# Moving three pieces at the two ends of layer 1: transposes of the second batch, the last norms and the range check

## The chip, the cores and the metric

The kernel runs on one core of a Trainium2 chip. The metric is the device time of one execution in microseconds. Engines are TensorE (PE; its weight loads PEld), VectorE (DVE), ScalarE (ACT), GpSimd (POOL) and SyncE (SP), which issues the DMAs here. Each engine works through its own queue in order and waits on semaphores that other engines raise.

## The reference

Two layers over x of shape (16, 1024, 256), all in float32. Layer 0 aggregates with a normalized adjacency matrix, applies two linear maps with batch norms, adds x and layer-normalizes. Layer 1, in which the change lies, is this, per batch, and a residual and a layer norm behind it:

```python
    def _L1_gnn_ref(x, para, adj, kv_w):
        B, N, C = x.shape
        ...
        c_adj = jnp.mean(fea, axis=1)
        diff = c_adj[:, None, :] - c_adj[:, :, None]
        A = jnp.abs(jnp.abs(jax.nn.sigmoid(diff) - 0.5) - 0.5) * 2.0
        A_s = (A + jnp.transpose(A, (0, 2, 1))) * 0.5
        Wg = adj[None, :, :] * A_s
        g = jnp.einsum('bcn,bnm->bcm', fea, Wg)
        g = jax.nn.relu(g * para.reshape(1, C, N))
        ...
        attn = jax.nn.softmax(jnp.einsum('bhnd,bhmd->bhnm', q, k) * scale, axis=-1)
        out = jnp.einsum('bhnm,bhmd->bhnd', attn, v)
    ...
    x = _layernorm(x + _L1_gnn_ref(x, L1_gnn_para, adj, L1_gnn_kv_w), axis=-1)
```

With q from the graph product g, k and v from x @ kv_w, and 4 heads of 64.

## The kernel before

Layer 0 ends at about 820 us; the rest is `fast()`, layer 1. Its order is written out in program order by a small planner, and each engine's queue follows that order.

**Steps and slots.** Attention of one batch is 16 steps: 2 halves of the queries (`hf`, 512 each), 2 pairs of heads, 4 groups of 256 keys. A step is `scores` (L783, TensorE), `exps` (L795, ScalarE), `sums` (L801, L804, VectorE, the softmax denominators' accumulator) and `attend` (L819, TensorE). With B = 16 that is steps 0 to 255. Two steps make a slot, so a batch has NC = 8 slots. `put(w, t, f, ...)` hangs a piece of side work on slot 8w + t, and the loop at the end (L1123) takes two slots at a time: first all pieces of both, in the order that `arrange` gives them, then four steps, with the scores and exponentials one step ahead. Pieces for batch b + 1 or b + 2 (norms, keys, values, graph product) hang on the slots of batch b. Slots -8 to -1 come before the first attention step; there `opening` also emits `gate0` and `graph0`, the gates and the graph product of batch 0, whose last call emits the four `queries`, which read the graph product from the two PSUM buffers of `ps_s`.

**First end (batch 1 in slots -8 to -1).** For each of four row blocks j: `load` (SP), `bn2_q` (POOL), `rows` and `ln1_a` (VectorE, then POOL), `ln1_b` (ScalarE, L642). `x1_t(1, j)` then transposes the block by four TensorE transposes (L671, tile `px`) and copies it on VectorE (L672, into `x1T`) for the keys and values of batch 1. `means` (L675, L677) and `crow` follow: `crow` transposes the row means (L692, tile `pc`), copies them (L694), and sends them through DRAM (L695, L696) to come back as a row on all partitions; the gates of batch 1 (`wg_a`, L706) read that row. `px`, `pc`, keys, values and the attention outputs share the four buffers of the pool `ps_t`.

**Last end (batch 15).** When a half is done, `dens` (L846, L848) and `recips` (L857, L859) make the reciprocals. `finish_a(15, j)` (L888 to L901) brings block j back to rows, scales it, adds the residual and takes norm statistics on VectorE and POOL; `finish_b(15, j)` (L909, L912) applies the norm on ScalarE and stores. For the second half (`by_pe`) the transposition back is four TensorE transposes per block (L885, tile `pf`), inside `finish_a`. `range_all` (L928 to L939) checks the range of the denominators: VectorE, a tiny matmul L935, VectorE; a rare general path follows it if the check fails. In the planner these lines set the places:

```python
                    if b == B - 1:
                        t_a, t_b = (t + 2 + k, t + 3 + k) if hf == 0 else (t + 1 + k, t + 2 + k)
```

where t is 4 for the first half and 8 for the second, k is 0 or 1. So before, `finish_b(15, 0)` is in slot 7 of batch 15 (127 over all), ahead of the last group of four steps, and `finish_b(15, 1)` in slot 128, behind them.

Of the kernel before, what the change touches and what calls it, by code (L numbers as in the profile page):

```python
# [9 lines left out]
F32 = mybir.dt.float32  # L10
# [6 lines left out]
P = 128  # L17
# [5 lines left out]
def gnn_norm_attention_kernel(  # L23
# [16 lines left out]
    nc = tc.nc  # L40
    B, N, C = x.shape
# [13 lines left out]
    ident = const.tile([P, P], F32, name="ident")  # L55
# [69 lines left out]
    with ExitStack() as l0:  # L125
# [32 lines left out]
        with ExitStack() as ph1:  # L158
# [9 lines left out]
            for i in range(0, NT, 2):  # L168
                t = hp.tile([P, 2, N], F32, tag="h", name=f"A{i}")
# [22 lines left out]
            KB = FB // P  # L192
# [6 lines left out]
            for h in range(NH):  # L199
# [11 lines left out]
                for j in range(NT):  # L211
                    p = ps.tile([P, FB], F32, tag="ah"[j % 2], name="pat")
# [25 lines left out]
            for c in range(HT):  # L238
                p = ps.tile([P, FB], F32, tag="a", name="pw1")
# [3 lines left out]
            for c in range(CT):  # L243
                p = ps.tile([P, FB], F32, tag="a", name="pw2")
# [142 lines left out]
            for f in range(HT):  # L387
                for h in range(NH):
# [3 lines left out]
                    p = hidden(B - 1, h, f)  # L392
# [57 lines left out]
        with ExitStack() as ph2:  # L450
# [74 lines left out]
            for k, pair in enumerate(pairs):  # L525
# [4 lines left out]
                if not ahead:  # L530
                    for j in range(LDP):
                        load(0, j)
                    for j in range(LDP, NT // 2):
                        t = accp.tile([P, 2, FB], F32, tag="acc", name=f"first{j}")
# [14 lines left out]
    NP = HEADS // 2  # L549
# [17 lines left out]
    def fast():  # L567
      with ExitStack() as fx:
# [13 lines left out]
        ps_t = pool("ps_t", 4, space=PSUM)  # L582

        x1s, x1Ts, css, crows, mvs, wgs = {}, {}, {}, {}, {}, {}
        kTs, qTs, vs, S, E, ACC, O, OT, DT = {}, {}, {}, {}, {}, {}, {}, {}, {}
# [222 lines left out]
        def by_pe(b, hf):  # L808
            return b == B - 1 and hf == NH - 1
# [42 lines left out]
        KB = FB // P  # L852
# [9 lines left out]

        OB = {}

        def fetch_o(b, j):
            hf, k = divmod(2 * j, KB)
            if by_pe(b, hf):
                return
            t = OB[b, j] = otp.tile([P, 2, C], F32, tag="ob", bufs=2, name=f"ob{b}_{j}")
            blk = o_dram[b, hf].rearrange("i (d e) (q n) -> q e (i d) n", e=Q, q=NQ)  # L870
            for q in range(NQ):
                nc.sync.dma_start(
                    t[q * Q : (q + 1) * Q].rearrange("p a (d n) -> p (a d) n", n=Q),
                    blk[q][:, ts(k // 2, 2 * C // Q), :],
                )

        def finish_a(b, j):
            hf, k = divmod(2 * j, KB)
            pool_r = (rp, "r") if b < B - 1 else (x1p, "x1")
            r = pool_r[0].tile([P, 2, C], F32, tag=pool_r[1], name=f"r_{b}_{j}")  # L880
            if by_pe(b, hf):
                p = ps_t.tile([P, 2, C], F32, tag="t", name="pf")
                for a in range(2):
                    for pair in range(NP):
                        nc.tensor.transpose(p[:, a, ts(pair, P)], OT[b, hf, pair][:, ts(k + a, P)], ident)  # L885
            else:
                p = r
                nc.vector.transpose(  # L888
                    r.rearrange("p a c -> p (a c)"), OB.pop((b, j)).rearrange("p a c -> p (a c)")
                )  # L890
            rd = RD[:, b * NT + 2 * j : b * NT + 2 * j + 2, :].rearrange("p a h -> p (a h)")
            nc.vector.tensor_mul(
                r.rearrange("p a (h d) -> p (a h) d", h=HEADS),
                p.rearrange("p a (h d) -> p (a h) d", h=HEADS),
                rd.unsqueeze(2).to_broadcast([P, 2 * HEADS, HD]),
            )
            nc.vector.tensor_add(r, r, x1s.pop((b, j)))
            mv, rs = ln_stats(sm, r, f"z{b}_{j}")
            nm = sm.tile([P, 2], F32, tag="nm", name=f"nm_{b}_{j}")
            for a in range(2):  # L900
                nc.gpsimd.tensor_scalar(  # L901
                    nm[:, a : a + 1], mv[:, a, 0:1], rs[:, a : a + 1], -1.0, op0=OP.mult, op1=OP.mult
                )
            R[b, j] = (r, rs, nm)
# [39 lines left out]
        NC = NS // 2  # L944
        at = {}

        def put(w, t, f, *a):
            at.setdefault(w * NC + t, []).append((f, a))
# [4 lines left out]
        for b in range(B):  # L953

            for hf in range(NH):
                t = (hf + 1) * (NC // NH)
                put(b, t, dens, b, hf)
                put(b, t, recips, b, hf)
                for k in range(KB // 2):
                    j = hf * (KB // 2) + k  # L960

                    t_a, t_b = (t + 2 + k, t + 6 + k) if hf == 0 else (t + 4 + k, t + 6 + k)
                    if b == B - 1:
                        t_a, t_b = (t + 2 + k, t + 3 + k) if hf == 0 else (t + 1 + k, t + 2 + k)
                    put(b, t + 1, fetch_o, b, j)
                    put(b, t_a, finish_a, b, j)
                    put(b, t_b, finish_b, b, j)
            if b == 0:
                continue

            put(b - 2, 2, begin, b)
            for j in range(NT // 2):
                put(b - 2, j, load, b, j)
                put(b - 2, j + 1, bn2_q, b, j)
                put(b - 2, j + 2, rows, b, j)
                put(b - 2, j + 2, ln1_a, b, j)
                put(b - 2, j + 3, ln1_b, b, j)
                if b == 1:
                    put(b - 2, j + 4, x1_t, b, j)
                    continue  # L980
                put(b - 2, j + 3, put_x1, b, j)
                put(b - 2, 5 + j // 2 * 2, get_x1, b, j)
                put(b - 2, min(6 + j, NC), x1_v, b, j)
            put(b - 2, NC - 2, means, b)
            put(b - 2, NC - 1, crow, b)

            i = 0
            for t, n in enumerate(WG):
                for i in range(i, i + n):
                    put(b - 1, t, gate, b, i)  # L990
                i += 1
            kv = [(keys, (b, c, h)) for h in range(NH) for c in range(CT)]
            kv += [(values, (b, j)) for j in range(0, NT, 2)]
            for t, n in enumerate(KV):
                for _ in range(n):
                    f, a = kv.pop(0)
                    put(b - 1, t, f, *a)
            m = 0
            for t, n in enumerate(QG):
                for m in range(m, m + n):  # L1000
                    put(b - 1, NC - len(QG) + t, graph, b, m)
                m += 1
        put(B - 1, 4, range_so_far)
        put(B - 1, NC + 1, range_all)

        nsteps = B * NS


        order = (dens, recips, x1_t, finish_a, fetch_o, finish_b, x1_v, rows, ln1_a, ln1_b, put_x1, get_x1, means, load, crow)
        rank = {f: k for k, f in enumerate(order)}  # L1010
        short = (dens, recips, x1_t)

        def is_short(fa):
            f, a = fa
            return f in short or f is finish_a and by_pe(a[0], 2 * a[1] // KB)

        long = (keys, values, graph)

# [9 lines left out]
        def arrange(pieces):  # L1028
            first = []
            gates = [fa for fa in pieces if fa[0] is gate]  # L1030
            many = [fa for fa in pieces if fa[0] in long]
            first += [fa for fa in pieces if fa[0] is bn2_q]
            alone = [fa for fa in pieces if fa[0] in (dens, recips, crow)]
            few = [fa for fa in pieces if fa not in first + gates + many + alone]
            few.sort(key=lambda fa: rank.get(fa[0], len(rank)))
            few_pe = [fa for fa in few if is_short(fa)]
            order = spread(many, few_pe) if len(many) < len(few_pe) else spread(few_pe, many)
            if few_pe and many and order[0][0] in long:
                order.remove(few_pe[0])
                order.insert(0, few_pe[0])  # L1040

            for fa in few:
                if not is_short(fa):
                    at_ = 0
                    for k, o in enumerate(order):
                        if o[0] in rank and rank[o[0]] <= rank.get(fa[0], len(rank)):
                            at_ = k + 1
                    order.insert(at_, fa)
            if any(fa[0] is graph for fa in many):
                order = gates + order  # L1050
            else:
                order = spread(order, gates)


            for f, k in ((dens, 1), (recips, 2)):
                k = ([n for n, fa in enumerate(order) if fa[0] in long] + [len(order)] * 3)[k]
                order[k:k] = [fa for fa in alone if fa[0] is f]
            return first + order + [fa for fa in alone if fa[0] is crow]


# [62 lines left out]
        for t in range(min(at) // 2, max(max(at) // 2, nsteps // NK - 1) + 1):  # L1123
# [3 lines left out]
            for k in range(len(now) + 1):  # L1127
                if k == behind and 0 <= g < nsteps:
                    sums(g)
                if k < len(now):  # L1130
                    f, a = now[k]
# [15 lines left out]
        )  # L1147

    flag = fast()


# [155 lines left out]
```

## Time and profile before

| | us |
|---|---|
| median of 3 runs | 2494.07 (2491.98 to 2497.5) |
| the profiled execution | 2492.39 |
| its span, first to last instruction | 2490.6 |
| PE busy | 2427.3 (97%) |
| DVE busy | 1798.8 (72%) |
| ACT busy | 1096.0 (44%) |
| POOL busy | 761.9 (31%) |
| mean granted TensorE clock | 0.993 of full |

The profile is of one execution. Times in the views are microseconds from the start of the span; L12 is line 12 of the kernel. A timeline line gives the start, the duration, engine, line, operation, tiles and shapes, the count of instructions merged into it, and in brackets how long the engine had been idle before it and what ended that. A view by windows gives, for each stretch, the busy time of each engine and the granted clock. A float32 matmul is recorded as two.

### The profile page before, as it was taken

The page shows a single profiled execution, that of the slowest core. Times are in us where ns is not written, and L with a number is a line of the kernel's source. Part 1 is how long each engine was busy: PE and PEld are TensorE (multiplying, and loading weights), DVE is VectorE, ACT ScalarE, POOL GpSimd, SP SyncE. Part 2 cuts the span into 40 slices and gives each one's busy share as a digit, 9 for nine tenths or more (in the row PEclk, how much of TensorE's full clock was granted, in tenths as well). Part 3 has the DMA queues.
Part 4 walks back from the last instruction along what each step waited for, and adds up shares of the span by engine and source line. Part 5 has one row for each costly group of instructions (what it writes and reads, how often), then busy time and mean ns, then how long its engine had stood idle before and what let it go on. Part 6 is the DMA issues. An engine that isn't in the chain of part 4 may idle for free. (4 is left out here: it accounts for less than half of the span.)

```text
span 2490.6 us, 33864 instructions
## 1 busy us (share of the span) xinstructions
PE 2427.3 (97%) x12341; PEld 1019.2 (41%) x12341; DVE 1798.8 (72%) x2552; ACT 1096.0 (44%) x1549; POOL 761.9 (31%) x826
## 2 busy tenths in 40 slices
PE   8999999999999799999999999999999999999996
PEld 4444444443444443443434434344344343443432
DVE  5545555555777577888788888888888878887666
ACT  2000000003543455564655656656556465564554
POOL 2222222221656232313223133232341432313002
PEclk9999999999999899999999999999999999999998
DMA  3122222222686443544554535445354455453211
GB/s 135 68 85 102 87 82 85 101 74 78 244 281 226 119 119 82 134 119 111 140 111 110 142 85 146 113 119 145 88 136 111 113 138 111 114 143 87 72 40 40
DMA packets 563118, 288.66 MB, mean 116 GB/s; under 512 B 390664, under 2 KB 535680, under 8 KB 555776
## 3 DMA queue, kind: packets, MB, share of 16 engines
q1 hardware_dynamic: 562944, 286.43, 41.6%
q8 instruction: 99, 1.62, 0.3%
q14 instruction: 75, 0.61, 0.1%
HBM read 192.43 MB, written 93.91 MB: 115 GB/s over the span
## 5 line engine op out<-in xcount | busy, mean ns | idle before, releaser
L795 ACT ACTIVATE e<-s 128x1024 f32<-128x1024 f32 x512 | 496.3, 1021 | 338.9 <-PE s L783 286.9
L804 DVE TENSOR_TENSOR acc<-acc,e 128x1024 f32<-128x1024 f32 x384 | 510.7, 1330 | 119.9 <-ACT e L795 93.3
L783 PE MATMUL s<-qT,kT 64*64 64x512 f32 x4096 | 492.3, 595 | 12.0 <-ACT e L795 8.7
L819 PE MATMUL o<-e,v 64*64 64x512 f32 x4096 | 485.3, 589 | 0.0
L757 PE MATMUL pg<-wg,x 128*128 128x512 f32 x960 | 428.9, 597 | 0.0
L610 POOL TENSOR_TENSOR yt<-yt,stq 128x512 f32<-128x512 f32 x120 | 179.4, 1495 | 430.3 <-DMA yt<-yT 390.3
L819 PEld LDWEIGHTS o<-e,v 64*64 64x64 f32 x4096 | 156.6, 133 | 283.5 <-issue 274.9
L783 PEld LDWEIGHTS s<-qT,kT 64*64 64x64 f32 x4096 | 147.3, 133 | 305.8 <-issue 261.3
L757 PEld LDWEIGHTS pg<-wg,x 128*128 128x128 f32 x960 | 177.5, 190 | 231.4 <-issue 227.5
L103 ACT COPY u<-pa 128x512 f32<-128x512 f32 x15 | 8.8, 586 | 475.3 <-PE pa L308 475.3
L716 DVE SCALAR_TENSOR_TENSOR wg<-wg,adj 128x1024 f32<-128x1024 f32 x128 | 162.9, 1302 | 4.0 <-ACT wg L709 1.2
L66 POOL TENSOR_SCALAR rs_z<-mv_z 128x2 f32<-128x2 f32 x64 | 16.9, 265 | 482.7 <-DVE mv_z L559 401.6
L308 PE MATMUL pa<-AhT,x 128*128 128x512 f32 x360 | 161.8, 592 | 0.0
L642 ACT ACTIVATE x<-x,nm_a,rs_a 128x256 f32<-128x256 f32 x128 | 75.8, 594 | 177.9 <-POOL nm_a L632 177.5
L831 DVE TENSOR_TENSOR ot<-o,ot 128x512 f32<-128x512 f32 x64 | 44.3, 692 | 149.8 <-ACT ot L830 149.8
L732 PE MATMUL pk<-x1T,kvw 128*128 128x512 f32 x256 | 122.2, 612 | 1.3 <-DVE x1T L672 1.3
L743 PE MATMUL pv<-kvw,x1T 128*128 128x256 f32 x512 | 117.1, 382 | 0.0
L66 POOL TENSOR_SCALAR rs_a<-mv_a 128x2 f32<-128x2 f32 x64 | 38.8, 606 | 252.9 <-DVE mv_a L559 233.5
L339 PE MATMUL ph<-agg,SW 128*128 128x512 f32 x240 | 112.8, 592 | 0.0
L743 PEld LDWEIGHTS pv<-kvw,x1T 128*128 128x128 f32 x512 | 96.0, 190 | 31.5 <-issue 16.5
L308 PE MATMUL pa<-T,sx 128*128 128x512 f32 x240 | 107.9, 592 | 0.0
L308 PEld LDWEIGHTS pa<-AhT,x 128*128 128x128 f32 x360 | 68.4, 190 | 86.1 <-issue 86.1
(192 smaller groups left out, 3155.1 us busy)
## 6 DMA issues: line engine op xcount, KB each, us to landing
adj<-in_adj_dram SPq DMA_DIRECT2D x128, 512.0 KB, 4.4
h<-hT SPq DMA_DIRECT2D x28, 1024.0 KB, 4.4
hL<-h SPq DMA_DIRECT2D x28, 1024.0 KB, 9.7
x<-in_x_dram SPq DMA_DIRECT2D x16, 1024.0 KB, 7.2
yT<-y SPq DMA_DIRECT2D x64, 256.0 KB, 2.5
out_dram<-r SPq DMA_DIRECT2D x64, 256.0 KB, 2.3
xr<-in_x_dram SPq DMA_DIRECT2D x62, 256.0 KB, 3.6
o<-ot SPq DMA_DIRECT2D x62, 256.0 KB, 2.3
```

Source lines behind the costliest of these rows:

```text
L308: nc.tensor.matmul(p, xs[n][:, k, :], bs[n][:, k, :], start=(k == 0), stop=(k == KN - 1))
L339: nc.tensor.matmul(p, ws[n][:, ts(f, P)], bs[n], start=True, stop=True)
L610: nc.gpsimd.tensor_tensor(y, y, sc, op)
L642: nc.scalar.activation(r, r, AF.Identity, bias=nm[:, a : a + 1], scale=rs[:, a : a + 1], accum_out=css[b][:, i : i + 1])
L716: nc.vector.scalar_tensor_tensor(t, t, 1.0, adjs[b * NT + i], op0=OP.add, op1=OP.mult)
L732: nc.tensor.matmul(p, kvw[:, k, ts(c, P)], x1Ts[b][:, k, ts(h, FB)], start=(k == 0), stop=(k == CT - 1))
L743: nc.tensor.matmul(p[:, ts(a, C)], x1Ts[b][:, k, ts(j + a, P)], kvw[:, k, C:], start=(k == 0), stop=(k == CT - 1),)
L757: nc.tensor.matmul(pg[b], x1s[b, k // 2][:, k % 2, ts(c, P)], wgs[b, k][:, ts(h, FB)], start=(k == 0), stop=(k == NT - 1))
L783: nc.tensor.matmul(t[r * HD : (r + 1) * HD, h, :], kTs[b, pair][h * HD : (h + 1) * HD, ts(2 * cb + r, HD)], qTs[b, pair, hf][h * HD : (h + ...
L795: nc.scalar.activation(E[g, a], S.pop((g, a)), AF.Exp)
L804: nc.vector.tensor_add(ACC[b, hf, pair], ACC[b, hf, pair], E[g, a])
L819: nc.tensor.matmul(O[b, hf, pair][r][h * HD : (h + 1) * HD, :], vs[b][r * HD : (r + 1) * HD, cb, pair * P + h * HD : pair * P + (h + 1) * HD],
```

## The change

Four things move, and nothing is added to or taken from the computation. `x1_t(1, j)` for all four blocks moves to slot -1, behind the last graph matmuls and the queries of batch 0. The transposes of `finish_a` for the last half become a piece of their own, `back`, which stands directly behind `dens` and ahead of `recips`. `finish_b(15, 0)` and `finish_b(15, 1)` move to slot 9 of batch 15 (129), behind all attention. `range_all` moves from slot 9 to slot 10, behind the last `finish_a`. Lines of the kernel after L870 are two to five higher in the changed one.

```diff
+        def back(b, j):
+            hf, k = divmod(2 * j, KB)
+            p = OB[b, j] = ps_t.tile([P, 2, C], F32, tag="t", name="pf")
+            for a in range(2):
+                for pair in range(NP):
+                    nc.tensor.transpose(p[:, a, ts(pair, P)], OT[b, hf, pair][:, ts(k + a, P)], ident)
+
         def fetch_o(b, j):
             hf, k = divmod(2 * j, KB)
-            if by_pe(b, hf):
-                return
...
             if by_pe(b, hf):
-                p = ps_t.tile([P, 2, C], F32, tag="t", name="pf")
-                for a in range(2):
-                    for pair in range(NP):
-                        nc.tensor.transpose(p[:, a, ts(pair, P)], OT[b, hf, pair][:, ts(k + a, P)], ident)
+                p = OB.pop((b, j))
...
                     if b == B - 1:
-                        t_a, t_b = (t + 2 + k, t + 3 + k) if hf == 0 else (t + 1 + k, t + 2 + k)
-                    put(b, t + 1, fetch_o, b, j)
+                        t_a, t_b = (t + 2 + k, NC + 1) if hf == 0 else (t + 1 + k, t + 2 + k)
+                    put(b, t if by_pe(b, hf) else t + 1, back if by_pe(b, hf) else fetch_o, b, j)
...
                 if b == 1:
-                    put(b - 2, j + 4, x1_t, b, j)
+                    put(b - 2, NC - 1, x1_t, b, j)
...
-        put(B - 1, NC + 1, range_all)
+        put(B - 1, NC + 2, range_all)
...
-        short = (dens, recips, x1_t)
+        short = (dens, recips, x1_t, back)
...
-            return f in short or f is finish_a and by_pe(a[0], 2 * a[1] // KB)
+            return f in short
...
-            alone = [fa for fa in pieces if fa[0] in (dens, recips, crow)]
+            alone = [fa for fa in pieces if fa[0] in (dens, back, recips, crow)]
...
-            for f, k in ((dens, 1), (recips, 2)):
+            for fs, k in (((dens, back), 1), ((recips,), 2)):
                 k = ([n for n, fa in enumerate(order) if fa[0] in long] + [len(order)] * 3)[k]
-                order[k:k] = [fa for fa in alone if fa[0] is f]
+                order[k:k] = [fa for fa in alone if fa[0] in fs]
```

In the built program this gives, at the first end, on TensorE: all 64 records of the graph, four times four transposes L671, L692, scores of step 0; on VectorE: `means`, the eight query instructions, four L672. At the last end, on TensorE: L846, eight transposes, L857; on VectorE: the reciprocal, two `finish_a`, the range check; on ScalarE: L848, then eight L909. The orders of POOL and SP are the same as before.

## The prediction

> **What bounds the kernel now.** I read the page first, then layer 1 by long windows, then the timeline at its two ends. The page and the windows say where time can be won at all:
>
> ```profile
> PE 2427.3 (97%) x12341; PEld 1019.2 (41%) x12341; DVE 1798.8 (72%) x2552; ACT 1096.0 (44%) x1549; POOL 761.9 (31%) x826
> ...
> 900.00:1300.00 400.00, 399.61 (x2556) 162.14 (x2548) 321.47 (x435) 227.50 (x315) 118.89 (x151) 1.00 0.47 115
> ...
> 2100.00:2454.00 354.00, 352.08 (x2390) 139.41 (x2386) 269.69 (x355) 202.84 (x268) 77.11 (x104) 1.00 0.37 91
> ```
>
> Columns are stretch, length, then busy us of PE, PEld, DVE, ACT, POOL, then granted clock. From 900 to 2454 TensorE has under 0.6% of gaps: nothing there absorbs a delay, so a shift J of the first end reaches the end of the span whole. The diff touches only the two ends. The first end, from the timeline (start, duration, instruction, and in brackets the idle time before it):
>
> ```profile
> 843.13 17.33 PE L1074 MATMUL pg<-wg,x 128*128 128x512 f32 x40
> ...
> 866.30 1.27 PE L671 MATMUL px<-ident,x 128*128 128x128 f32 x4 [5.84 <-ACT x L642]
> ...
> 873.92 0.69 DVE L672 COPY x1T<-px 128x512 f32<-128x512 f32 x1 [3.06 <-PE px L671]
> ...
> 881.46 0.27 PE L692 MATMUL pc<-ident,cs 128*8 128x128 f32 x1
> ...
> 884.50 0.68 DVE L672 COPY x1T<-px 128x512 f32<-128x512 f32 x1
> ...
> 887.67 1.15 ACT L706 ACTIVATE wg<-crow,hcs 128x1024 f32<-128x1024 f32 x1 [1.31 <-DVE acc L801]
> ...
> 898.49 2.00 PE L783 MATMUL s<-qT,kT 64*64 64x512 f32 x16 [0.84 <-ACT e L795]
> ```
>
> See that the graph matmuls of batch 0 stall 5.84 us for batch 1's rows, but that what finally restarts TensorE in earnest is a chain: L692, the row's way through DRAM, the gates L706 on ScalarE, and then scores of step 2. The last end:
>
> ```profile
> 2446.33 7.86 DVE L804 TENSOR_TENSOR acc<-acc,e 128x1024 f32<-128x1024 f32 x6
> ...
> 2460.88 1.33 ACT L909 ACTIVATE r<-r,nm,rs_z 128x256 f32<-128x256 f32 x2 [6.38 <-POOL nm L901]
> ...
> 2463.14 2.56 DVE L804 TENSOR_TENSOR acc<-acc,e 128x1024 f32<-128x1024 f32 x2
> 2463.16 3.51 PE L783 MATMUL s<-qT,kT 64*64 64x512 f32 x16 [7.82 <-ACT e L795]
> ...
> 2473.47 1.07 PE L846 MATMUL pd<-acc,ones 128*32 128x512 f32 x8
> ...
> 2480.01 0.19 PE L935 MATMUL pflag<-mm,ones 128*1 128x2 f32 x2 [3.24 <-DVE mm L933]
> 2480.13 1.11 PE L885 MATMUL pf<-ident,ot 128*128 128x128 f32 x4
> ...
> 2481.29 0.69 DVE L892 TENSOR_TENSOR r<-pf,RD 128x512 f32<-128x512 f32 x1 [0.72 <-PE pf L885]
> ```
>
> ScalarE stands in front of step 253's exponentials with a norm whose factor is not there (6.38), TensorE waits for those exponentials (7.82), and later for the range check (3.24).
>
> **The last end, step by step** (times on the axis of before). ScalarE's L909 of (15,0) goes behind the attention, so step 253's exponentials start when the earlier norms end, 2454.50, instead of 2462.11. TensorE then runs steps 253 to 255 at its usual 3.43 us per step and ends attention at about 2464.1 instead of 2473.5. This 9.4 us does not come back, because VectorE is the next one late: its queue holds both finish_a of slots 126 and 127 until 2463.04 in either kernel, with no idle time from 2446.33 on but 0.22 us, and the six sums L804 of steps 253 to 255 only after them. Six back to back cost 7.86 (the row at 2446.33, with the same small POOL work beside them); bounds are 7.68 (three pairs at 2.56) and 9.21 (the six at 898.47, beside large POOL work). I take 7.86: accumulator done at 2470.9, against 2473.0 before. The denominators L846 of the second pair start there; those of the first pair are already done, so half of the eight are left.
>
> TensorE will have been idle 6.3 us by then. After the 7.82 us gap before, 16 matmuls took 3.51 us instead of 1.90, and the granted clock was 0.50 in 2460 to 2466; after the 3.24 us gap four transposes took 1.11 instead of 0.60. So I price this tail at half clock: L846's rest 1.07 (0.53 at full clock), to 2472.0; L831 hides below it on VectorE (0.69, to 2471.6). Now the added order tells: the eight transposes of back come before L857 on TensorE. At half clock they take 2 x 1.07 (start to start at 866.30), to 2474.1, and cover ScalarE's L848 (0.59, to 2472.6). L857 takes 1.11, the reciprocal starts at 2475.2, the first L892 at 2475.5, 0.04 and 0.25 us after their causes as now. Before it was 2476.81: 1.3 won. At full clock: transposes to 2472.6, L857 to 2473.3, L892 at 2473.6, 3.2 won.
>
> The first row block takes 2.61 on VectorE (2476.81 to the range check at 2479.42) and the second one 2.69 (2481.29 to 2483.98). Between them now lie 1.87 us of check, flag matmul and transposes; with the check behind and the transposes done, all of it goes. Second block done at 2475.5 + 2.61 + 2.69 = 2480.8 against 2483.98: **3.2 us won**, 5.1 at full clock, 1.8 with the slow sums. From there POOL, ScalarE and the store to 2490.6 stay as they are. Edits at nothing: the range check costs 1.15 us behind 2480.8 and is over at 2482.0, while POOL and ScalarE need until 2483.4 for the last norm; without that cover it would cost at most these 1.15. The two moved norms (2 x 1.09 on ScalarE) lie from 2472.6 to 2474.8, behind L848 and 5 us ahead of the next norm, which would pay up to 2.2 otherwise; on SP their two stores keep their place, with only the last two stores behind them.
>
> **The first end.** All four transpositions of batch 1 go behind batch 0's graph, whose 64 matmuls run on from 843.13 at 0.433 each to 870.9 instead of 881.1. Only one thing that mattered waited for that: rows of block 3, held on VectorE by a copy L672 that waited 3.06 for TensorE. They start when POOL is done, 872.2 instead of 874.5, and the chain behind them (POOL, L642, means) brings the queries from 880.26 to 877.95, their end from 884.59 to 882.3. But the four L672 now stand behind the eight query instructions, and in the built program L692 waits for the first L672, since the four px tiles hold all four PSUM buffers of their pool. First L672: 882.2 to 882.9. So L692 starts at 882.9 instead of 881.46, and queued behind it on TensorE are scores of step 0 and the keys, on SP (L695, L696) the loads for batch 2. The chain from L692 over DRAM to L706, and ScalarE's unbroken run from there to step 1's exponentials, moves by 1.45: step 2's scores at 899.9 instead of 898.49. The profile names VectorE's sum L801 as releaser of L706, done 0.06 before it; if that and not the row is the true one, J is 1.2.
>
> The clock adds a little: TensorE has only small transposes from 870.9 to 882.9, so scores 0 and the keys begin at half clock. The row: restarted at 866.30, the clock was 0.50 until about 872.3, 6.0 us; restarted at 2463.16, until about 2466.4, 3.2 us. Work from 883.2 to step 0's last attention matmul is 13.8 us at full clock (scores 0 and 1 and attention 0 at 1.71 each, keys 6.9, values 1.7), plus half of the cold time, 1.6 to 3.0: step 2 at 898.6 to 900.0 by TensorE alone, about the same as by the row's chain, and together, as key copies and gates interleave on ScalarE, up to 900.7. J is 0.2 to 2.2; I take **+1.7**.
>
> The Trainium skill, TensorE: Matmul & The Clock Gate, section "Why this matters for your kernels", speaks against this change: it asks for no TensorE gap over about 3 us between bursts, and the change makes two where there was one of 5.84 and one of 7.82. Its Part 1 gives about 3.4 us of sustained work to get the clock back; the row at 866.30 shows 6.0. By the page alone J would be about 1.5, an estimate from its 3.4 us; by the row up to 2.2.
>
> **The sum.** 3.2 less 1.7 is 1.5 us: span 2490.6 to 2489.1, and with the 1.8 us around it (2492.39 less 2490.6) 2490.9. The profiled execution lies 1.7 under the median 2494.07, so the forecast for a median is 2494.07 - 1.5 = **2492.6**.
>
> **Rivals.**
> - The waits come back whole: 5.84 + 7.82 + 3.24, some 17 us, 2477. Against it: VectorE's queue and the chain over L642 and L692, which no part of the diff shortens. 0.03.
> - The tail stays at full clock: 5.1 won, J at 1.2 or below: 2490.2 or less. It needs the clock to hold over 6.3 us of idle; the row fell 4.2 us after the last matmul at 2455.34, and 5.1 us after 860.46. 0.12.
> - Slower, at the row's way through DRAM: L692's row now leaves 1.45 us later and may run into the loads for batch 2 and the gates' matrix rows, whose DMA share is 0.6 to 1.0 from 885 on. Its way took 5.6 us (882.05 to 887.67); if that doubles, J is 7.3 and the kernel 2498.2. It loses from the point where the way takes 1.5 us longer. For it: the DMA share. Against it: the loads stand behind it on the same SP queue. 0.10.
> - VectorE's sums at 1.53 each as at 898: the tail gives 1.8, the sum is 0: 2494.0. 0.12.
>
> The forecast, inside +-1.5 us, has 0.63. About 0.2% (5 us) is what a measurement of this kernel can tell from no change; its three runs spread over 5.5. Faster than that takes the first rival, or the second with a low run: 0.11. Slower takes half of the third, with a high run: 0.06. Within: 0.83. The range runs from the second rival less about 1.5 us of run scatter, 2488.7, to the fourth plus 2.5 of scatter and part of the third, 2496.5.
>
> **What would show it.** Right: no wait of TensorE for L795 near 2462; six L804 back to back, and L846's second half just behind them, after some 6 us of TensorE idle; a granted clock of 0.50 from then to the end; L892 twice without a wait between; the graph of batch 0 in one piece of 27.8 us; L692 right behind the first of four L672. Wrong: L804 with waits in between (then VectorE is not the bound of the tail), the tail's transposes at 0.6 for four, or step 2's scores no later after 843.13 than now (55.4 us).

## The result, and the profile after

The changed kernel takes 2492.35 us, the median of 4 runs (2491.44 to 2493.48). The kernel before takes 2495.78 beside it (4 runs, 2491.98 to 2498.09). The ratio is 0.9988, with a 95% interval of 0.9971 to 1.0005: no difference that these runs can tell. The forecast was 2492.6 and "within 0.2%". Beside the later experiments the kernel before had medians of 2493.26, 2492.53 and 2493.92 (13, 15 and 18 runs), so the 2495.78 lies high, and the 3.4 us between the two medians here say little.

What moved is below the scatter of the times, so it is read from the traces. Every time below is counted from an instruction that both kernels have. The program is cut at four of them: the first graph matmul of batch 0, the start of step 2's scores, the copy L831 behind step 251, and the end of the last norm on ScalarE.

| stretch | before | after | difference |
|---|---|---|---|
| start of the span to the graph of batch 0 | 843.13 | 844.68 | +1.55 |
| first end: graph to step 2's scores | 55.36 | 56.51 | +1.15 |
| middle: to L831 behind step 251 | 1555.62 | 1555.66 | +0.04 |
| last end: to the end of the last norm | 32.54 | 29.73 | -2.81 |
| from there to the end of the span | 3.97 | 4.60 | +0.63 |
| span | 2490.6 | 2491.2 | +0.6 |

The first row is not the change's: over all thirteen kernels of this study the graph of batch 0 starts between 843.07 and 845.2, and nothing ahead of it differs. The other four rows sum to -1.0 us. The changed kernel's profiled execution has the longer span, though its last end is 2.8 us shorter; spans alone would have misled.

Of the changed kernel, first the engines' line of the page, then the same two long windows as before (stretch, length, busy time of PE, PEld, DVE, ACT, POOL, granted clock, DMA share, GB/s):

```profile
PE 2431.7 (98%) x12341; PEld 1020.6 (41%) x12341; DVE 1799.9 (72%) x2552; ACT 1097.8 (44%) x1549; POOL 764.1 (31%) x826
```

```profile
900.00:1300.00 400.00, 399.46 (x2566) 161.01 (x2559) 320.54 (x434) 228.09 (x315) 120.06 (x151) 1.00 0.47 116
2100.00:2454.00 354.00, 352.05 (x2390) 139.28 (x2384) 267.86 (x355) 202.37 (x264) 78.97 (x104) 1.00 0.37 91
```

The middle is as full as it was. PE shows 4.4 us more busy time for the same 12341 instructions, and the matmuls below that run at half clock (3.61 and 1.92 for what took 1.90 and 1.05) show where such time comes from. It is no extra work, and PE's share says nothing on gain or loss here.

The first end, from the timeline of the changed kernel:

```profile
844.68 27.63 PE L1076 MATMUL pg<-wg,x 128*128 128x512 f32 x64
...
878.81 1.27 PE L671 MATMUL px<-ident,x 128*128 128x128 f32 x4 [1.52 <-ACT x L642]
...
883.90 2.48 DVE L672 COPY x1T<-px 128x512 f32<-128x512 f32 x4
884.64 0.38 PE L692 MATMUL pc<-ident,cs 128*8 128x128 f32 x1 [4.56 <-DVE x1T L672]
...
885.06 3.61 PE L783 MATMUL s<-qT,kT 64*64 64x512 f32 x16
...
890.32 1.15 ACT L706 ACTIVATE wg<-crow,hcs 128x1024 f32<-128x1024 f32 x1 [0.55 <-DMA crow<-crow_d]
...
901.19 2.00 PE L783 MATMUL s<-qT,kT 64*64 64x512 f32 x16
```

The graph runs in one piece and ends 10 us earlier, but L692 now waits for the first of the four copies L672. Scores of step 0 follow at half clock (3.61 for 16, against 1.90). L706 now names the row's DMA as its releaser. Step 2 comes 56.51 after the graph's start, 1.15 later than before.

The last end, from the timeline of the changed kernel:

```profile
2457.17 1.91 ACT L795 ACTIVATE e<-s 128x1024 f32<-128x1024 f32 x2
...
2465.71 7.87 DVE L804 TENSOR_TENSOR acc<-acc,e 128x1024 f32<-128x1024 f32 x6
...
2473.63 1.92 PE L846 MATMUL pd<-acc,ones 128*32 128x512 f32 x4 [5.57 <-DVE acc L804]
2475.48 1.97 PE L870 MATMUL pf<-ident,ot 128*128 128x128 f32 x8
...
2477.24 1.06 PE L857 MATMUL pr<-ident,dt 128*128 128x128 f32 x4
...
2478.64 0.69 DVE L894 TENSOR_TENSOR r<-pf,RD 128x512 f32<-128x512 f32 x1
...
2481.25 0.66 DVE L894 TENSOR_TENSOR r<-pf,RD 128x512 f32<-128x512 f32 x1
...
2485.49 1.09 ACT L911 ACTIVATE r<-r,nm,rs_z 128x256 f32<-128x256 f32 x2 [1.48 <-POOL nm L903]
```

The waits of ScalarE for L901 (6.38) and of TensorE for L795 (7.82) are gone. Their place takes one of TensorE for VectorE's six sums (5.57). The two row blocks follow each other without a wait.

### The profile page after: what moved, and what is told of

It reads as the page before. It is cut to its first block, busy times and chain, and to the rows that moved or that the text cites. A ratio compares the mean times of both kernels' runs of the same rounds, so it can differ in the third digit from the quotient of the medians.

```text
span 2491.2 us, 33861 instructions
## 1 busy us (share of the span) xinstructions
PE 2431.7 (98%) x12341; PEld 1020.6 (41%) x12341; DVE 1799.9 (72%) x2552; ACT 1097.8 (44%) x1549; POOL 764.1 (31%) x826
## 5 line engine op out<-in xcount | busy, mean ns | idle before, releaser
L795 ACT ACTIVATE e<-s 128x1024 f32<-128x1024 f32 x512 | 496.8, 1022 | 336.9 <-PE s L783 282.0
L819 PE MATMUL o<-e,v 64*64 64x512 f32 x4096 | 485.3, 589 | 0.0
L819 PEld LDWEIGHTS o<-e,v 64*64 64x64 f32 x4096 | 156.6, 133 | 282.8 <-issue 274.3
L831 DVE TENSOR_TENSOR ot<-o,ot 128x512 f32<-128x512 f32 x64 | 44.3, 692 | 148.0 <-ACT ot L830 148.0
```

Source lines behind the costliest of these rows:

```text
L795: nc.scalar.activation(E[g, a], S.pop((g, a)), AF.Exp)
L819: nc.tensor.matmul(O[b, hf, pair][r][h * HD : (h + 1) * HD, :], vs[b][r * HD : (r + 1) * HD, cb, pair * P + h * HD : pair * P + (h + 1) * HD],
```

## The experiments

The theory was the prediction's: at the last end VectorE's queue is the bound, so that only 1.3 of the 7.8 us of TensorE's wait come back, the rest of the gain being the 1.87 us between the row blocks; at the first end the rows' copies behind the queries hold L692. The rivals: the 7.8 us wait comes back whole; the first end costs nothing, or it is not L692 but TensorE's half clock that sets it. Kernels for which no time is given ran once and are read from their traces.

**first_end_alone**: before, with only the transposes moved.

```diff
-                    put(b - 2, j + 4, x1_t, b, j)
+                    put(b - 2, NC - 1, x1_t, b, j)
```

> The kernel before with the second batch's transposes alone moved behind the graph product and the queries. First end, from the start of the graph matmuls to the start of step 2's scores: 55.36 us before, 56.51 in the changed kernel. Theory (the row of means waits for a copy that stands behind the queries on VectorE, and its chain sets step 2): 56.2 to 57.3, with the small transpose L692 right after the first of four copies. Rival (the stall of 5.84 us in the graph comes back): 50 or less. Last end, from L831 of step 251 to the end of the last L909: 32.5 as before, by either.

Measured: first end 56.12 (before 55.36), last end 32.36 (before 32.54): the first end alone is later, by 0.8 against this trace of before, and the last end is as it was. Time 2493.46 (one run; before 2493.26 beside it).

**norms_alone**: before, with only the two norms moved.

```diff
-                        t_a, t_b = (t + 2 + k, t + 3 + k) if hf == 0 else (t + 1 + k, t + 2 + k)
+                        t_a, t_b = (t + 2 + k, NC + 1) if hf == 0 else (t + 1 + k, t + 2 + k)
```

> The kernel before with the norms of (15,0) and (15,1) alone moved behind the attention. Last end (32.54 us before, 29.73 changed): theory (VectorE's queue holds the sums until its two finish_a are through, and TensorE's clock is down by then) 31.0 to 31.6, so 1.0 to 1.5 won of the 7.8 that TensorE no longer waits; TensorE done with attention some 9 us earlier, then idle for over 5. Rival (the wait comes back whole): 24.7. First end 55.4 by either.

Measured: last end 31.22. The timeline of norms_alone:

```profile
2460.72 3.61 PE L819 MATMUL o<-e,v 64*64 64x512 f32 x32
...
2462.97 7.86 DVE L804 TENSOR_TENSOR acc<-acc,e 128x1024 f32<-128x1024 f32 x6
...
2470.88 1.92 PE L846 MATMUL pd<-acc,ones 128*32 128x512 f32 x4 [5.57 <-DVE acc L804]
```

Attention is over before the sums have well begun, and TensorE then waits 5.57 for them. From L831 of step 251 to the last sum it is 16.72 us, against 18.89 in before and 16.73 in the changed kernel: 2.17 earlier. The stretch from there to the end of the last norm grew by 0.85, since TensorE's first work behind its wait runs at half clock (L846 takes 1.92). So of a wait of 7.82, taken away whole, 1.3 reached the end.

**back_and_check_alone**: the change without the other two parts.

```diff
-                        t_a, t_b = (t + 2 + k, NC + 1) if hf == 0 else (t + 1 + k, t + 2 + k)
+                        t_a, t_b = (t + 2 + k, t + 3 + k) if hf == 0 else (t + 1 + k, t + 2 + k)
...
-                    put(b - 2, NC - 1, x1_t, b, j)
+                    put(b - 2, j + 4, x1_t, b, j)
```

> The kernel before with the piece back and the later range check alone; norms and first end as before. Last end (32.54 us before): theory (the clock is full again here, since scores and attention of three steps come just before; only the 1.87 us between the two row blocks go, and the transposes ahead of L857 cost nothing beside the copy L848) 30.5 to 30.9. Rival (the transposes ahead of L857 hold up the reciprocal): 31.0 to 31.7. The stall of 7.8 us stays by either.

Measured: last end 31.85, a miss by 1 us. Behind the last sum it is 11.64 us (31.85 less 20.21), against 13.65 in before: 2.0 won, as the theory has it, so the transposes ahead of L857 hold nothing up. What missed lies ahead of that: the last sum came at 20.21, though nothing ahead of it is changed. The timeline of back_and_check_alone shows step 253 and 254 behind the wait:

```profile
2465.61 3.69 PE L783 MATMUL s<-qT,kT 64*64 64x512 f32 x16 [7.81 <-ACT e L795]
...
2469.08 3.09 PE L819 MATMUL o<-e,v 64*64 64x512 f32 x16
```

L819 takes 3.09 where before took 1.89: after the same wait the clock stayed at half for 5.9 us, not 3.2. The last section tells why.

**check_alone**: before, with only the range check moved.

```diff
-        put(B - 1, NC + 1, range_all)
+        put(B - 1, NC + 2, range_all)
```

> The kernel before with one edit: the range check goes behind the last row block. Theory A (the check, issued last, is what makes the stretch after the last norm longer): from the last L831 of step 251 to the end of the last norm 30.5 to 30.9 us instead of 32.54, since the 1.87 us of check, flag matmul and transposes between the two row blocks go; the accumulator as in before, 18.9, unless the half clock lies otherwise; after the last norm 4.5 to 4.7 instead of 3.95. Together 1.0 to 1.5 won. Theory B (the transposes' own place, or the moved norms, make it longer): after the last norm 3.9 to 4.0, together 1.6 to 2.1 won. The first end as in before within its scatter, 53.7 to 56.9.

Measured: last end 30.66 (1.88 won), the last sum at 18.90, after the last norm 4.59, together 1.26 won: theory A. The timeline of check_alone, around the two row blocks:

```profile
2478.85 0.69 DVE L892 TENSOR_TENSOR r<-pf,RD 128x512 f32<-128x512 f32 x1 [0.18 <-PE pf L885]
...
2481.46 0.66 DVE L892 TENSOR_TENSOR r<-pf,RD 128x512 f32<-128x512 f32 x1
...
2485.03 0.15 DVE L939 TENSOR_TENSOR badi<-bad 1x1 int32<-1x1 f32 x1
...
2485.70 1.09 ACT L909 ACTIVATE r<-r,nm,rs_z 128x256 f32<-128x256 f32 x2 [1.48 <-POOL nm L901]
```

The second row block starts 2.61 after the first one instead of 4.48, with the check's place alone; `back` is not needed for this. But the stretch behind the last norm grows by 0.62, as it does in the changed kernel, so it is the check's place that lengthens it.

What ends the program can be read from the traces. In all thirteen kernels the last instruction comes 1.39 us after the last store has landed, whether the check is early or late. In the three with the check between the row blocks and the tail as in before (before, first_end_alone, norms_alone) that store lands 2.42 to 2.56 us after its issue; in the nine with the check last it lands 3.12 to 3.37 after it. For before and the changed kernel this is 2.56 and 3.19, which is the whole 0.63. The flag `badi` is done 6.1 to 6.4 us before the end in the nine and about 10 in the three, but TensorE's branch on it is over at 2489.62 in the changed kernel, ahead of the landing at 2489.80.

What lies beside the store differs. The DMA queues of the two kernels from 2486.6 to 2489.9, the time of the last store (packets, MB, share of the 16 engines), first before, then changed:

```profile
q1 hardware_dynamic: 272, 0.26, 23.8%
q14 instruction: 5, 0.04, 3.9%
```

```profile
q1 hardware_dynamic: 272, 0.26, 26.5%
q14 instruction: 5, 0.04, 3.6%
q8 instruction: 1, 0.02, 2.4%
```

The same 272 packets of the store share the time with one packet of q8 (16 KB, of kind `instruction`). In all nine kernels with the check last this packet starts 0.14 to 0.49 us behind the store's issue; in the three it is over before the issue. That it is what slows the store fits these times, but no run moves it alone, so it is not shown.

**first_end_undone**: the change with the transposes where they were.

```diff
-                    put(b - 2, NC - 1, x1_t, b, j)
+                    put(b - 2, j + 4, x1_t, b, j)
```

> The changed kernel with the transposes of the second batch put back among the graph matmuls. First end 55.4 us (56.51 changed), last end 29.7 as changed. So by the theory 1.1 us faster than the changed kernel and 2.8 faster than the kernel before: ratio 0.9985 to 0.999 against before. Rival (the first end gains, the tail does not): slower than the changed kernel.

Measured: 2490.63 (10 runs, 2488.56 to 2494.7), before 2493.26 beside it, ratio 0.9992, interval 0.9982 to 1.0001: not told from before. In its trace the last end is 29.67, the changed kernel's; the first end is 53.68, 1.7 below that of before with the same order. That scatter belongs to the account of the first end, and the expected 55.4 was missed by it. Five kernels have the old order there: 53.68, 54.04, 55.27, 55.36, 56.86, mean 55.04. Four have the change's: 56.12, 56.13, 56.33, 56.51, mean 56.27. The order costs 1.2 on average, -0.7 to +2.8 from one trace to another. The scatter is the old order's: there the graph ends 36.40 to 38.71 behind its start, L692 follows, and the row's way from L695 to L706 takes 5.40 to 6.47, while in the four the graph ends at 27.63 in each, L692 comes at 39.42 to 39.96, and the way takes 4.98 to 5.21. In all nine, step 2 comes 10.81 to 10.88 behind the first gate L706, so what reaches L706 late reaches step 2.

**copies_between**: the change, with three blocks' transposes behind the graph and ahead of all queries, the fourth between the two halves of the queries, and the means behind them.

```diff
-                    put(b - 2, NC - 1, x1_t, b, j)
...
-            put(b - 2, NC - 2, means, b)
+            put(b - 2, NC - 1 if b == 1 else NC - 2, means, b)
...
-                for h in range(NH):
-                    for c in range(CT):
-                        queries(0, c, h, PG0[h][:, c, :])
+                for j in range(3):
+                    x1_t(1, j)
+
+        def between():
+            for h in range(NH):
+                for c in range(CT):
+                    queries(0, c, h, PG0[h][:, c, :])
+                if h == 0:
+                    x1_t(1, 3)
+
+        put(-1, NC - 1, between)
```

> The changed kernel with VectorE's order at the first end altered: three of the four copies of the second batch's transposes ahead of the means, the fourth between the second and third query, so that the row of means no longer waits behind all queries. First end (55.36 us before, 56.51 changed): theory (that wait was the loss) 54.0 to 55.8; L692 some 3 us earlier after the graph's start than changed (39.96). Rival (the loss is TensorE's lowered clock over scores and keys): 56.5 or more. Last end 29.7 as changed.

Measured: first end 54.85, 1.66 below the changed kernel's. L692 comes 34.62 after the graph's start, 5.3 earlier than in the changed kernel (some 3 were expected), and L706 3.7 earlier, but step 2 only 1.66. The timeline of copies_between shows who is late next:

```profile
880.85 1.99 PE L783 MATMUL s<-qT,kT 64*64 64x512 f32 x8 [1.16 <-DVE qT L765]
...
883.57 1.98 PE L783 MATMUL s<-qT,kT 64*64 64x512 f32 x8 [0.73 <-DVE qT L765]
...
885.48 8.56 PE L732 MATMUL pk<-x1T,kvw 128*128 128x512 f32 x16
```

Scores and keys, now started earlier in the half clock, take 4 us and 8.56, and the rest follows without a gap on TensorE. So both theories hold, one behind the other: with the copies out of the way, step 2 no longer follows L706 by 10.8 us but by 12.95, and TensorE's own work, part of it at half clock, is what it waits for. The size is less sure than 1.66 looks: this order's four traces (the three kernels built on it below included) have first ends of 54.59 to 55.38, mean 54.89, which is 1.4 below the changed order's mean and about that of the old order.

**norm_in_gap**: the change, with `finish_a(15, 1)` moved from slot 127 to 128, behind the six sums, where VectorE has slack.

```diff
-                        t_a, t_b = (t + 2 + k, NC + 1) if hf == 0 else (t + 1 + k, t + 2 + k)
+                        t_a, t_b = (t + 2 if k == 0 else NC, NC + 1) if hf == 0 else (t + 1 + k, t + 2 + k)
```

> The changed kernel with finish_a of (15,1) moved behind the sums of the last steps, so that VectorE works on it while TensorE makes the last denominators. Last end (29.73 us changed): theory (VectorE's queue sets when the last sums end, and VectorE idles 4.16 us later) 25.7 to 26.5. Rival (TensorE's lowered clock or the chain of denominators is the bound and nothing is won by earlier sums): 29 or more. First end 56.5 as changed.

Measured: last end 25.38, a little less than expected and 4.35 below the changed kernel's. The timeline of norm_in_gap:

```profile
2465.59 2.56 DVE L804 TENSOR_TENSOR acc<-acc,e 128x1024 f32<-128x1024 f32 x2 [0.47 <-DVE acc L804]
2468.20 1.05 PE L846 MATMUL pd<-acc,ones 128*32 128x512 f32 x4 [2.17 <-DVE acc L804]
2469.18 1.09 PE L870 MATMUL pf<-ident,ot 128*128 128x128 f32 x8
2470.11 0.60 PE L857 MATMUL pr<-ident,dt 128*128 128x128 f32 x4
...
2472.01 0.23 DVE L859 RECIPROCAL RD<-pr 128x16 f32<-128x16 f32 x1
```

The last sum is done at 13.32 instead of 16.73, so 3.41 came from VectorE's queue: this shows that it was the bound. The other 0.94 lies behind the sum. TensorE's wait is down to 2.17, L846, the transposes and L857 run at full speed and are over at 2470.71, and the reciprocal then waits only for VectorE's own `finish_a(15, 1)`. Its one run took 2486.70.

**clock_kept**: the change, with six matmuls whose result nobody reads ahead of the second pair's denominators.

```diff
+                if pair == 1 and by_pe(b, hf):
+                    w = ps_t.tile([P, FB], F32, tag="t", name="warm")
+                    for _ in range(6):
+                        nc.tensor.matmul(w, ident, qTs[b, 1, hf], start=True, stop=True)
```

> The changed kernel with six extra matmuls of 128x512, whose result nobody reads, on TensorE between the two pairs' denominators, 5.2 us in TensorE's idle time. Last end (29.73 us changed): theory (the tail's 14 us run at half clock, which costs about 2) 27.2 to 28.0, with L846's rest at 1.0 instead of 1.92, eight transposes at 1.0 instead of 1.97, L857 at 0.66 instead of 1.06, and a granted clock of 1.00 there. Rival (these lie beside VectorE's work): 29.7.

Measured: last end 27.56, 2.17 below the changed kernel's, with the last sum at the same 16.73. The timeline of clock_kept:

```profile
2467.97 5.42 PE L847 MATMUL warm<-qT,ident 128*128 128x512 f32 x12
2473.62 1.05 PE L850 MATMUL pd<-acc,ones 128*32 128x512 f32 x4 [0.23 <-DVE acc L804]
2474.60 1.09 PE L874 MATMUL pf<-ident,ot 128*128 128x128 f32 x8
```

The six matmuls fill the wait to within 0.23, and everything behind them takes about half the time. So the half clock costs this tail 2.17 us.

**both_ends**: copies_between and norm_in_gap together.

> copies_between and norm_in_gap together. First end 54.0 to 55.8 us, last end 25.7 to 26.5, so 1 to 2 us and 3.3 to 4 us under the changed kernel, and some 6 us, ratio 0.997 to 0.998, under the kernel before. Rival (gains at the ends do not add up, since something between absorbs them): a stretch between the two ends longer than the 1555.7 us of both kernels.

Measured: 2487.07 (11 runs, 2485.85 to 2488.19), before 2492.53 beside it; ratio 0.9975, interval 0.9966 to 0.9984. This is a gain that the runs can tell, and it lies in the last end: 25.69 against 32.54. The first end, 55.38, is where it was before, and the middle, 1555.52, absorbs nothing. The last end is 0.31 longer than in norm_in_gap; here L846 fell into half clock again (1.92).

**both_early_check**: both_ends with the range check back in slot 129, between the row blocks.

```diff
-        put(B - 1, NC + 2, range_all)
+        put(B - 1, NC + 1, range_all)
```

> both_ends with the range check back between the two row blocks. Theory A (the late check costs 0.65 after the last norm, and early it costs VectorE its 1.15 between the row blocks): last end 26.7 to 27.0 instead of 25.69, after the last norm 3.9 to 4.0 instead of 4.59, together 0.4 to 0.6 slower than both_ends, not to be told from it by times. Theory B (the late check costs nothing after the last norm): 4.5 to 4.7 there, 1.1 to 1.3 slower in sum. Theory C: the flag's matmul waits for the check on VectorE and holds the second block's transposes as in before; in this order they are done before it, so nothing of the 1.87 beyond the 1.15 should return; if it does, last end 27.5.

Measured: last end 26.79 (+1.10), after the last norm 4.25 (-0.32). The transposes of the second block were done before the check here, so it costs VectorE its own 1.1 and no more. The time is 2486.7 (8 runs; ratio 0.9972, interval 0.9961 to 0.9982), not told from both_ends. Theory A by its signs, but only 0.32 of the 0.65 came back. The trace says where the rest is: the last store lands 2.84 us after its issue, between the 2.56 of before and the 3.16 of both_ends, and the q8 packet ends 0.85 us after that issue.

**both_kept**: both_ends with the six matmuls of clock_kept.

> both_ends with the six filler matmuls of clock_kept ahead of the second pair's denominators. Theory A (the half clock still costs the tail after the accumulator: 12.4 us there in both_ends, 10.8 in clock_kept): last end 24.0 to 24.6 instead of 25.69, the rest as in both_ends, ratio to before 0.9965 to 0.9975. Rival: with the sums 3.4 us earlier TensorE's idle stretch is short, the clock falls at another window edge, or the fillers themselves stand before the denominators: 25.2 to 25.9, no gain.

Measured: last end 27.27, 1.58 longer than in both_ends; 2489.02 (11 runs), ratio 0.9982, interval 0.9973 to 0.9991. The rival's second case. The timeline of both_kept:

```profile
2466.27 2.55 DVE L804 TENSOR_TENSOR acc<-acc,e 128x1024 f32<-128x1024 f32 x2 [0.47 <-DVE acc L804]
2466.64 5.42 PE L847 MATMUL warm<-qT,ident 128*128 128x512 f32 x12
...
2471.99 1.05 PE L850 MATMUL pd<-acc,ones 128*32 128x512 f32 x4
```

The sums are done at 2468.82, and the denominators stand behind fillers until 2471.99. What was free in a wait of 5.57 costs 3.2 in one of 2.17.

## Why the prediction was right

It was right in its number and mostly for its reasons, with two terms mis-sized and one priced at nothing wrongly. To compare, 2.74 is taken off the times of the last end after (2456.85 against 2454.11 at L831 of step 251).

- **Where TensorE's wait goes.** Exponentials of step 253: 2454.4 measured, 2454.50 predicted; attention over: 2464.3, 2464.1; last sum: 2470.8, 2470.9. The six sums took 7.87, the value chosen. norms_alone and norm_in_gap show from both sides that VectorE's queue decides; this step was right to 0.2.
- **The tail behind it at half clock.** Right in kind (clock_kept: 2.17 for it), mis-sized in one term. L846's rest was priced at 1.07, as half of the row of eight (1.07) at twice its time. But four of them take 1.05 alone at full clock, and 1.92 here: the row of eight was no sum of eight. L857 therefore came late, though less than that, since the transposes between cost 1.76 and not 2.14. First L894: 2475.9, predicted 2475.5.
- **The row blocks.** 2.61 apart, as predicted; check_alone shows that the check's place alone does it. The last end as a whole gave 2.8, predicted 3.2: the 0.4 is what L857 came late.
- **"The range check costs nothing."** Wrong, by 0.63. The prediction set the check's end against the end of the last norm, which indeed is later, and held that "POOL, ScalarE and the store to 2490.6 stay as they are". The store did not: it landed 3.19 us after its issue instead of 2.56, and the program ends 1.39 behind its landing in both. That the move of the check does it is shown by check_alone; what slows the store is not. The bound that the prediction gave, 1.15 without cover, holds by its size, though it was meant for VectorE's work.
- **The first end.** L692 right behind the first copy, the half clock of scores 0, the row's DMA as releaser of L706: all there. J was +1.7 within 0.2 to 2.2; measured 1.15 in this pair of traces and 1.2 on average. L692 came 1.63 later after the graph's start, where 1.45 was predicted. But the row's way from L695 to L706, which the prediction held at its 5.62, took 4.98, and that is the term that was mis-sized: in the four kernels with the change's order it takes 4.98 to 5.21, in the five with the old one 5.40 to 6.47. Why it is shorter is open. The 0.25 that J had for the clock did not show either: step 2 follows L706 by 10.87, against 10.82. The other case that the prediction named, the sum L801 as releaser of L706 in before, is not so: in all nine kernels L706 starts 0.10 to 0.11 behind the last landing of the row, in before too, and in some of them ahead of the sum's end.
- **The sum.** -2.81, +1.15 and +0.63 make -1.0 against -1.5 predicted. The rivals: waits whole, refuted by norms_alone; the row's way through DRAM, which took 5.0 us (L695 at 885.34 to L706 at 890.32) where 5.6 was the price and 11.2 the fear; slow sums, refuted by 7.87; full clock, refuted by 1.92. That the measured 2492.35 lies only 0.25 from 2492.6 is luck in part: errors of +0.4, -0.55 and +0.63 partly cancel, and runs of one kernel scatter by 2 to 6 us.

The warning about gaps of TensorE that the prediction cites from the Trainium skill (TensorE: Matmul & The Clock Gate, "Why this matters for your kernels") was to the point: clock_kept puts its price at 2.17 us at the last end. No run here removes the half clock from the first end alone.

## What to carry to other kernels

A wait that vanishes from the busiest engine is worth only the distance to the engine that is late next: here the sums came 2.2 of 7.8 us earlier, of which 1.3 reached the end, and the way to the rest was to move work in that engine's queue (both_ends: 0.25% of the whole, where the change itself could not be told from nothing). Work moved "behind everything" can lengthen what comes after it: look at the stretch from the last result to the end of the program, too. Filling a wait with spare matmuls won 2.17 us where the fill of 5.4 was shorter than the wait (5.57), and lost 1.58 where it was longer (2.17).

## What the runs showed of the hardware

The granted clock changes on a fixed grid. These are windows of the kernel before, cut at the edges that a fine scan of the granted clock gave (the last three columns are the granted clock, the DMA share and GB/s):

```profile
865.50:872.30 6.80, 6.00 (x10) 2.80 (x11) 4.13 (x11) 2.55 (x8) 6.28 (x11) 0.50 0.40 84
872.40:876.00 3.60, 3.60 (x13) 1.86 (x12) 2.02 (x4) 1.27 (x4) 1.27 (x4) 1.00 0.00 0
2456.00:2459.50 3.50, 0.00 (x0) 0.00 (x0) 3.26 (x8) 0.00 (x0) 0.07 (x1) 1.00 0.07 22
2459.50:2466.30 6.80, 3.14 (x16) 1.04 (x20) 5.54 (x9) 4.05 (x5) 4.86 (x6) 0.50 0.12 40
```

Half-clock stretches are about 6.8 us long here, 10.2 in the changed kernel's first end and in back_and_check_alone's last: multiples of 3.41. The edges at 865.5, 872.3, 2459.5, 2466.4 and 2480.0 lie 0, 2.0, 467.0, 469.0 and 473.0 times 3.413 from the first; in the other kernels too every edge falls on such a grid to 0.03, over 1600 us, with an offset of its own in each execution. The Trainium skill, TensorE: Matmul & The Clock Gate, Part 1, has this rule: a free-running window of 4096 cycles, 3413 ns, and about one busy window to get the clock back. The runs agree, and add the size: after a stall the full clock came 3.2 to 3.5 us after the restart where TensorE restarted within 0.25 us of an edge (before at 2463.16, first_end_undone at 866.53, norms_alone at 868.01), and 5.9 to 6.1 where it restarted 0.8 to 1.0 behind one (before at 866.30, back_and_check_alone at 868.00 and 2465.61). Two more lie between: first_end_alone restarted at 2464.40, 0.56 behind an edge, and had the full clock after 2.85; check_alone at 868.21, 0.64 behind one, after 6.18. It is as if only a window that TensorE fills from nearly its beginning counted; this is an inference from these restarts, and no run moves a restart against the grid. It fits the prediction's two rows, 6.0 and 3.2, which it could only take as a range, part of the first end's scatter (the eight graph matmuls behind the stall took 4.69 to 6.14 us), and the last sum's 20.21 in back_and_check_alone.

The middle, 1555 us of attention, took 1555.5 to 1555.7 in all thirteen kernels. Where a stretch without gaps repeats to 0.01%, differences of one microsecond at the ends can be read from single traces; the times of whole runs, with 2 to 6 us of scatter, could not have told them.
